# A post-norm decoder layer in float32: self-attention's division by the softmax sums moved from GpSimd to ScalarE, and a third buffer for rows of projections

## The chip, the cores and the metric

The kernel runs on one core of a Trainium2 chip. The metric is the time of one execution on the device, in microseconds (us). A core has five engines that work side by side, each through its own queue of instructions in order: TensorE (PE; its weight loads are listed as PEld), VectorE (DVE), ScalarE (ACT), GpSimd (POOL) and SyncE (SP, which here only issues DMAs). SBUF is the working memory on the core, PSUM the memory that TensorE writes its results to, DRAM the large memory outside.

## The reference, cut to what matters

Eight sequences of 256 tokens with 1024 features each go through one layer, all in float32. The layer is self-attention, cross-attention to a context, and a memory block, each followed by a residual sum and a layer norm:

```python
x = layernorm(x + self_attention(x))       # 32 heads of 32, 8 key/value heads, rope, causal
x = layernorm(x + cross_attention(x, ctx)) # 32 heads of 128, 8 key/value heads, rope, mask
x = layernorm(x + memory(x))               # router, top 8 of 256 slots, gate
```

The change touches the softmax of self-attention:

```python
attn = einsum('bhqd,bhkd->bhqk', q, k) * scale + causal
attn = softmax(attn, axis=-1)              # exp(a - max) / sum
out  = einsum('bhqk,bhkd->bhqd', attn, v)
```

## The kernel before

**Stages.** `run` calls `self_attention`, `cross_attention` and `tail`. Self-attention takes the first 1.3 ms of 3.7. Cross-attention needs keys and values projected from the context, and sums of blocks of its weights (it multiplies in Strassen's way, with seven products where eight would be plain). Both are made during self-attention, as filler for TensorE: `seven` (L625) makes the seven products p1 to p7, and `sums_of_inputs` and `sums_of_outputs` (L379, L397) let GpSimd add and subtract weight blocks (`combine`, L376 and L377) and write them to DRAM (L393, L413).

**Steps.** Self-attention runs 64 steps. Step s = 8b + c takes sequence b and chunk c of four heads. In step s the loop at L443 emits, in this order for TensorE:

- `transposed(s, 0)` to `transposed(s, 3)` (L283): three transposes per head of the softmax weights into one PSUM buffer `tr` (there is one), and a copy `at` out of it, by VectorE for heads 0 and 2, by ScalarE for heads 1 and 3 (L292). Between them lie single filler products (`one`) and `query(s + 2)`;
- `scores(s + 1)` (L241): the products of queries and keys of the next step, and their softmax;
- `others(s)` (L360): for c below 4 and b above 0 the output projection of the sequence before (L332), for c from 4 and b from 1 to 6 the keys (L195) or values (L223) of the next sequence. With c = 5 and 6 also `turn`, the transposes of the normed rows (L351), whose result ScalarE's queue writes to DRAM as `x1T` (L358);
- `weighted(s)` (L295): weights by values, and the copy `sa_oT` (L310) by VectorE;
- the rest of the filler. Steps 4 to 59 have four products of filler each.

TensorE's order is the one in which the program is written (`manual_schedule(engines={PE})`). On the other engines a scheduler of the language places the instructions, and each engine then runs its own in order.

**PSUM buffers.** Projections, outputs and filler products share three `mm` buffers in rotation. A product may start when the third allocation before it has been read by whoever copies it: ScalarE copies projections of queries and keys (`sa_raw`, L200), values (`sa_v`, L227) and the filler's first products (`half`, L665), VectorE the others.

**The softmax of a step.** The four heads form two tiles `att` of 128 x 2 x 384: for each head, 128 weights of the first block of queries and 256 of the second. For each of the eight parts VectorE takes scores, mask and maximum in one instruction (L265), and ScalarE the exponential with its sum (L270). For each tile VectorE forms the reciprocals of four sums (`rec`, L274), and GpSimd multiplies, two instructions per tile, each over both heads:

```python
rec = rec.rearrange("p (j t) -> p j t", t=2)
for i, (lo, hi) in enumerate(((0, 128), (128, 384))):
    nc.gpsimd.tensor_tensor(
        att[:, :, lo:hi], att[:, :, lo:hi],
        rec[:, :, i : i + 1].to_broadcast([P, 2, hi - lo]), ALU.mult,
    )
```

GpSimd's queue also holds the weight sums (L377), the last addition of rope (L623), the power in the layer norm (`ln_rstd`, L130), and DMA issues: residual rows (L117), rows of the position table (L572), keys (L722) and values (L727) on their way to DRAM.

**`raw`.** In `seven` VectorE assembles each result of 128 x 512 in a tile `raw` (L657), with two buffers. For keys and queries rope reads it. For values it is written to DRAM as it stands, by a DMA from GpSimd's queue, and its buffer is free when that write has landed.

Of the kernel before, what the change touches and what calls it, by code (L numbers as in the profile page):

```python
# [8 lines left out]
F32 = mybir.dt.float32  # L9
I32 = mybir.dt.int32  # L10
U32 = mybir.dt.uint32
AF = mybir.ActivationFunctionType
ALU = mybir.AluOpType
# [5 lines left out]
P = 128  # L19
# [16 lines left out]
TQ = 512  # L36
# [32 lines left out]
class Layer:  # L69
# [70 lines left out]
    def self_attention(self):  # L140
# [4 lines left out]
        nc, tc, a, uni, small = self.nc, self.tc, self.a, self.uni, self.small  # L145
# [95 lines left out]
        def scores(s):  # L241


            b, c = divmod(s, KC)
            qT, kT = qTs.pop(s), kTs[b]
            scs = [p_sc.tile([P, 2, 512], F32, name="sc") for _ in range(2)]
            for lo, hi, q0 in ((0, 128, 0), (128, 384, 128)):
                for j in range(4):
                    r = 32 * j
                    nc.tensor.matmul(  # L250
                        scs[j // 2][:, j % 2, lo:hi],
                        lhsT=qT[r : r + 32, q0 : q0 + P],
                        rhs=kT[r : r + 32, c // 4, 0 : hi - lo],
                        start=True, stop=True,
                    )
            atts[s] = []
            for sc in scs:
                att = sp.tile([P, 2, 384], F32, name="att", bufs=4)
                nmax = small.tile([P, 4], F32, name="nmax")
                sums = small.tile([P, 4], F32, name="sums")  # L260
                rec = small.tile([P, 4], F32, name="rec")
                parts = [(jj, lo, hi) for jj in range(2) for lo, hi in ((0, 128), (128, 384))]
                for i, (jj, lo, hi) in enumerate(parts):

                    nc.vector.tensor_tensor_reduce(  # L265
                        out=att[:, jj, lo:hi], in0=sc[:, jj, lo:hi], in1=mask[:, 256 - (hi - lo) :],
                        scale=-SA_SCALE, scalar=BIG, op0=ALU.add, op1=ALU.min,
                        accum_out=nmax[:, i : i + 1],
                    )
                    nc.scalar.activation(  # L270
                        att[:, jj, lo:hi], att[:, jj, lo:hi], AF.Exp,
                        bias=nmax[:, i : i + 1], scale=-1.0, accum_out=sums[:, i : i + 1],
                    )
                nc.vector.reciprocal(rec, sums)  # L274
                rec = rec.rearrange("p (j t) -> p j t", t=2)
                for i, (lo, hi) in enumerate(((0, 128), (128, 384))):
                    nc.gpsimd.tensor_tensor(  # L277
                        att[:, :, lo:hi], att[:, :, lo:hi],
                        rec[:, :, i : i + 1].to_broadcast([P, 2, hi - lo]), ALU.mult,
                    )  # L280
                atts[s].append(att)

# [154 lines left out]
        values(0, 0)  # L437
        query(1)
        scores(0)
        values(0, 1)  # L440
        last = SA_STEPS
        later = None
        for s in range(last):  # L443
# [34 lines left out]
            if s + 1 < last:  # L478
                scores(s + 1)
# [145 lines left out]
    def seven(self, name, m, xb, turned, done, eager=False):  # L625

        nc = self.nc
        now = {}  # L630
        if eager:
            now["a"] = self.weights([P, KC, XA_D], self.a[name][2 * m])

        def product(w, block):
            ps = self.mm()
            rhs = xb()[block]
            if turned:
                for t in range(2):
                    for k in range(4):
                        nc.tensor.matmul(  # L640
                            ps[:, t * P : (t + 1) * P], lhsT=rhs[:, k, t * P : (t + 1) * P], rhs=w[:, k, :],
                            start=(k == 0), stop=(k == 3),
                        )
            else:
                for k in range(4):
                    nc.tensor.matmul(  # L646
                        ps[:, :S], lhsT=w[:, k, :], rhs=rhs[:, k, :], start=(k == 0), stop=(k == 3)
                    )
            return ps[:, :S]

        def add(out, in0, in1):
            nc.vector.tensor_tensor(out, in0, in1, ALU.add)  # L652

        def half():
            return self.hp.tile([P, S], F32, name="half", bufs=4)

        def raw():  # L657
            return self.uni.tile([P, TQ], F32, name="raw", bufs=2)

        def p1():  # L660
            if not eager:
                now["a"] = self.weights([P, KC, XA_D], self.a[name][2 * m])
            ps = product(now["a"][:, :4, :], "B11")
            now["p1"] = half()
            nc.scalar.copy(now["p1"], ps)  # L665

        def p2():
            ps = product(now["a"][:, 4:, :], "B21")
            now["c1"] = raw()
            add(now["c1"][:, :S], ps, now["p1"])  # L670

        def p6():
            now["s24"] = self.weights([P, KC, XA_D], self.wsums[name, m][0])
            ps = product(now["s24"][:, :4, :], "T2")
            now["u2"] = half()
            add(now["u2"], ps, now["p1"])

        def p7():
            now["s31"] = self.weights([P, KC, XA_D], self.wsums[name, m][1])
            ps = product(now["s31"][:, :4, :], "T3")  # L680
            now["u3"] = half()
            add(now["u3"], ps, now["u2"])

        def p5():
            ps = product(now["s31"][:, 4:, :], "T1")
            now["c2"] = raw()
            add(now["u2"], ps, now["u2"])
            add(now["c2"][:, S:], ps, now["u3"])

        def p3():  # L690
            ps = product(now["s24"][:, 4:, :], "B22")
            add(now["c1"][:, S:], ps, now["u2"])
            done(0, now["c1"])

        def p4():
            w = self.weights([P, 4, XA_D], self.a[name][2 * m + 1][:, 4:, :])
            ps = product(w, "T4")
            add(now["c2"][:, :S], ps, now["u3"])
            done(1, now["c2"])

        return [p1, p2, p6, p7, p5, p3, p4]
# [680 lines left out]
```

## Time and profile before

| what | value |
|---|---|
| runs | 3705.0, 3705.7, 3714.4 us (median 3705.7) |
| the profiled execution's own time | 3709.3 us |
| its span, first to last instruction | 3707.5 us |
| mean granted TensorE clock | 0.974 of full speed |
| GpSimd's divisions (L277) | 256 instructions, 211.9 us |
| ScalarE's exponentials (L270) | 512 instructions, 225.3 us |
| SP's queue waiting for writes of `x1T` | 88.1 us, 13 times |

The profile is one execution taken by the hardware profiler. A group of instructions is given by its line in the kernel, its engine and operation, what it writes and reads, its number, its busy time, the mean duration of one in ns, and the idle time of the engine before it with what ended that. A line of waits says who waited for whom, for how many us in all, how often, and the longest. A line of the timeline gives the start in us, the duration, the engine and the instruction, and in brackets how long the engine had been idle and what released it. A line of windows gives, for a stretch of the span, its length, then the busy time and number of instructions on PE, PEld, DVE, ACT and POOL, the mean granted clock, the share of DMA time and GB/s. TensorE's records count two matmuls for one of the program in float32, transposes apart. The granted clock is TensorE's[...].

### The profile page before, as it was taken

How to read it: one execution, taken by the hardware profiler on the slowest of the kernel's cores; microseconds unless marked ns; L12 is line 12 of the kernel's file. 1: busy time of each engine (PE TensorE's matmuls, PEld its weight loads, DVE VectorE, ACT ScalarE, POOL GpSimd, SP SyncE). 2: the span in 40 equal slices, each digit the busy share in tenths (PEclk: the TensorE clock that was granted, in tenths of full speed). 3: DMA queues.
4: the chain of work that ended last, by engine and by line, in shares of the span. 5: the costliest groups of instructions: out<-in, count | busy, mean ns of one | idle time of the engine just before them, and what ended most of it. 6: DMA issues, size and time to landing. Idle time of an engine off the chain costs nothing.

```text
span 3707.5 us, 48946 instructions
## 1 busy us (share of the span) xinstructions
PE 3556.7 (96%) x17422; PEld 2614.0 (71%) x17422; DVE 2059.2 (56%) x5874; ACT 943.3 (25%) x2905; POOL 982.0 (26%) x1007
## 2 busy tenths in 40 slices
PE   6999999899999889999999999999999999999997
PEld 5777777676768657777777777777767777777764
DVE  4555555554655444555565555656565566455567
ACT  2322222222222213222222222222222222222223
POOL 4445454545544211111121111211111111111110
PEclk8999999999999989999999999999999999999996
DMA  7547575756665353333433333432433443333322
GB/s 263 181 168 256 196 264 209 248 195 226 241 218 177 118 203 116 123 120 117 150 125 127 119 109 120 149 129 100 136 112 120 141 132 117 122 112 117 117 87 114
DMA packets 220642, 574.18 MB, mean 155 GB/s; under 512 B 21104, under 2 KB 57264, under 8 KB 218992
## 3 DMA queue, kind: packets, MB, share of 16 engines
q1 hardware_dynamic: 173504, 461.26, 37.6%
q0 software_dynamic: 22528, 77.61, 5.6%
q10 hardware_dynamic: 24368, 32.18, 2.4%
q8 instruction: 139, 2.28, 0.2%
q14 instruction: 103, 0.84, 0.1%
HBM read 478.31 MB, written 92.67 MB: 154 GB/s over the span
## 4 chain that ended last, share of the span: by engine, by line
PE 66%; DVE 4%; POOL 1%; DMA 1%; issue 1%; ACT 1%; SPq 0%; POOLq 0%; ACTq 0%; DVEq 0%
PE mm L646 20%; PE mm L844 19%; PE sc L746 6%; PE mm L795 5%; PE tr L779 3%; PE mm L332 2%; PE mm L195 2%; PE mm L1079 2%; PE mm L640 1%; PE mm L1219 1%; PE mm L1073 1%; PE mm L899 1%; PE tr L287 1%; POOL acc L872 0%; DVE res L872 0%
## 5 line engine op out<-in xcount | busy, mean ns | idle before, releaser
L646 PE MATMUL mm<-x1T,w 128*128 128x256 f32 x3584 | 846.4, 381 | 10.8 <-DMA w<-xa_wq_sums 5.8
L646 PEld LDWEIGHTS mm<-x1T,w 128*128 128x128 f32 x3584 | 672.9, 191 | 102.5 <-issue 15.1
L623 POOL TENSOR_TENSOR qT<-qT,t 128x512 f32<-128x512 f32 x128 | 162.8, 1272 | 1120.9 <-DVE t L622 855.0
L844 PE MATMUL mm<-w,xoS 128*128 128x512 f32 x992 | 447.7, 594 | 0.0
L760 ACT ACTIVATE xatt<-xatt,nmax 128x256 f32<-128x256 f32 x512 | 255.5, 500 | 489.3 <-DVE nmax L755 477.2
L652 DVE TENSOR_TENSOR raw<-mm,half 128x256 f32<-128x256 f32 x384 | 161.5, 421 | 378.4 <-PE mm L646 310.0
L844 PE MATMUL mm<-w,xoT 128*128 128x512 f32 x744 | 335.1, 593 | 0.0
L652 DVE TENSOR_TENSOR half<-mm,half 128x256 f32<-128x256 f32 x288 | 121.6, 422 | 359.3 <-PE mm L646 300.9
L844 PEld LDWEIGHTS mm<-w,xoS 128*128 128x128 f32 x992 | 181.4, 190 | 182.8 <-issue 174.9
L277 POOL TENSOR_TENSOR att<-att,rec 128x256 f32<-128x256 f32 (+1 forms) x256 | 211.9, 849 | 332.2 <-DVE rec L274 325.9
L746 PE MATMUL sc<-kT,qT 128*128 128x256 f32 x1024 | 264.5, 382 | 6.9 <-POOL qT L623 6.7
L270 ACT ACTIVATE att<-att,nmax 128x128 f32<-128x128 f32 (+1 forms) x512 | 225.3, 441 | 147.9 <-DVE nmax L265 147.9
L795 PEld LDWEIGHTS mm<-xat,v 128*128 128x128 f32 x1024 | 194.0, 190 | 81.8 <-issue 57.9
L195 PE MATMUL mm<-xT,w 128*128 128x256 f32 x1024 | 245.3, 395 | 0.0
L795 PE MATMUL mm<-xat,v 128*128 128x256 f32 x1024 | 242.4, 379 | 1.5 <-ACT xat L784 1.5
L640 PE MATMUL mm<-w,ctxT 128*128 128x128 f32 x1792 | 227.0, 284 | 10.7 <-ACT sa_v L227 10.1
L844 PEld LDWEIGHTS mm<-w,xoT 128*128 128x128 f32 x744 | 138.9, 190 | 138.6 <-issue 119.9
L332 PE MATMUL mm<-sa_wo,sa_oT 128*128 128x512 f32 x512 | 229.8, 602 | 0.0
L640 PEld LDWEIGHTS mm<-w,ctxT 128*128 128x128 f32 x1792 | 216.8, 199 | 17.2 <-ACT sa_v L227 11.5
L810 POOL TENSOR_TENSOR xoS<-xoT 128x512 f32<-128x512 f32 x62 | 78.5, 1266 | 567.9 <-ACT xoT L804 567.9
L784 ACT COPY xat<-tr 128x512 f32<-128x512 f32 x256 | 148.0, 582 | 308.3 <-PE tr L779 308.0
L755 DVE CUSTOM_DVE_ANT_0 xatt<-sc,bias 128x256 f32<-128x256 f32 x512 | 196.4, 420 | 45.2 <-PE sc L746 38.8
(198 smaller groups left out, 5068.0 us busy)
## 6 DMA issues: line engine op xcount, KB each, us to landing
w<-in_xa_wo SPq DMA_DIRECT2D x129, 512.0 KB, 4.0
w<-xa_wq_sums SPq DMA_DIRECT2D x128, 512.0 KB, 3.4
w<-xa_wo_sums SPq DMA_DIRECT2D x124, 512.0 KB, 3.4
w<-in_xa_wq SPq DMA_DIRECT2D x96, 512.0 KB, 3.5
w<-in_sa_wq SPq DMA_DIRECT2D x64, 512.0 KB, 6.7
sa_wo<-in_sa_wo SPq DMA_DIRECT2D x64, 512.0 KB, 6.0
w<-xa_wk_sums SPq DMA_DIRECT2D x32, 512.0 KB, 4.6
w<-xa_wv_sums SPq DMA_DIRECT2D x32, 512.0 KB, 5.7
```

Source lines behind the costliest of these rows:

```text
L195: nc.tensor.matmul(ps[:, :S], lhsT=lhs[:, k, :], rhs=xT[:, k, :], start=(k == 0), stop=(k == KC - 1),)
L270: nc.scalar.activation(att[:, jj, lo:hi], att[:, jj, lo:hi], AF.Exp, bias=nmax[:, i : i + 1], scale=-1.0, accum_out=sums[:, i : i + 1],)
L277: nc.gpsimd.tensor_tensor(att[:, :, lo:hi], att[:, :, lo:hi], rec[:, :, i : i + 1].to_broadcast([P, 2, hi - lo]), ALU.mult,)
L332: nc.tensor.matmul(ps, lhsT=oTs[b * KC + c][:, tt * P : (tt + 1) * P], rhs=wos[b, half][c // 2][:, c % 2, :], start=(c == 0), stop=(c == K ...
L640: nc.tensor.matmul(ps[:, t * P : (t + 1) * P], lhsT=rhs[:, k, t * P : (t + 1) * P], rhs=w[:, k, :], start=(k == 0), stop=(k == 3),)
L646: nc.tensor.matmul(ps[:, :S], lhsT=w[:, k, :], rhs=rhs[:, k, :], start=(k == 0), stop=(k == 3))
L652: nc.vector.tensor_tensor(out, in0, in1, ALU.add)
L746: nc.tensor.matmul(sc[:, qt, :], lhsT=qT[:, q0 : q0 + P], rhs=kT[:, b * S : (b + 1) * S], start=True, stop=True,)
L755: nc.vector.tensor_tensor_reduce(out=att[:, qt, :], in0=sc[:, qt, :], in1=self.bias[:, 2 * b + qt, :], scale=-XA_SCALE, scalar=BIG, op0=AL ...
L760: nc.scalar.activation(att[:, qt, :], att[:, qt, :], AF.Exp, bias=nmax[:, qt : qt + 1], scale=-1.0, accum_out=sums[:, qt : qt + 1],)
L795: nc.tensor.matmul(po[:, b * S : (b + 1) * S], lhsT=self.v[G][:, NB * b + kt, :], rhs=at[:, kt * S : (kt + 1) * S], start=(kt == 0), stop= ...
L844: nc.tensor.matmul(ps, lhsT=oT[lhs][:, u, off + p * P : off + (p + 1) * P], rhs=w[:, u, :], start=(u == 0), stop=(u == 1),)
```

## The change

ScalarE multiplies by the reciprocals, with an Identity activation whose scale is the column of `rec`: four instructions per tile, one per head and block of queries, in place of GpSimd's two. And `raw` has three buffers in place of two.

```diff
@@ -272,11 +272,9 @@
                 nc.vector.reciprocal(rec, sums)
-                rec = rec.rearrange("p (j t) -> p j t", t=2)
-                for i, (lo, hi) in enumerate(((0, 128), (128, 384))):
-                    nc.gpsimd.tensor_tensor(
-                        att[:, :, lo:hi], att[:, :, lo:hi],
-                        rec[:, :, i : i + 1].to_broadcast([P, 2, hi - lo]), ALU.mult,
+                for i, (jj, lo, hi) in enumerate(parts):
+                    nc.scalar.activation(
+                        att[:, jj, lo:hi], att[:, jj, lo:hi], AF.Identity, bias=0.0, scale=rec[:, i : i + 1]
                     )
                 atts[s].append(att)
@@ -655,7 +653,7 @@
         def raw():
-            return self.uni.tile([P, TQ], F32, name="raw", bufs=2)
+            return self.uni.tile([P, TQ], F32, name="raw", bufs=3)
```

## The prediction

> **What bounds the kernel now.** I read the page first (parts 1 and 2), then the waits, then the timeline of single steps of self-attention.
>
> ```profile
> PE 3556.7 (96%) x17422; PEld 2614.0 (71%) x17422; DVE 2059.2 (56%) x5874; ACT 943.3 (25%) x2905; POOL 982.0 (26%) x1007
> ...
> 100.00:1330.00 1230.00, 1150.66 (x7349) 890.11 (x7349) 667.79 (x2089) 324.87 (x1228) 562.56 (x635) 0.97 0.60 209
> ...
> L277 POOL TENSOR_TENSOR att<-att,rec 128x256 f32<-128x256 f32 (+1 forms) x256 | 211.9, 849 | 332.2 <-DVE rec L274 325.9
> ...
> PE tr L287 <- DVE at L292: 41.0, 21, 9.8
> ...
> PE tr L287 <- POOL att L277: 29.0, 21, 6.3
> ```
>
> TensorE sets the end: busy for 96% of the span. The windows line gives 100 to 1330 us, most of self-attention: PE 1150.7 of 1230 us (so 79 us idle), ACT 325, POOL 563. ScalarE has room by its sum, GpSimd is the fuller one. So the change is worth what it does to PE's idle time there (about 102 us from 25 to 1330 us, adding PE's gaps along the timeline) and nothing else. Of that, 29.0 us ended when a GpSimd division landed, 41.0 us when VectorE emptied the one `tr` buffer.
>
> The second reading is of one step with filler. It shows what ScalarE must do in time:
>
> ```profile
> 614.57 0.94 PE L250 MATMUL sc<-sa_kT,sa_qT 32*128 32x128 f32 x16
> 615.44 3.72 PE L195 MATMUL mm<-xT,wk 128*128 128x256 f32 x16
> 616.81 0.40 ACT L270 ACTIVATE att<-att,nmax 128x128 f32<-128x128 f32 x1 [1.60 <-DVE nmax L265]
> 617.12 0.19 ACT L270 ACTIVATION_READ_ACCUMULATOR att<-att,nmax 128x1 f32 x1
> 617.21 0.49 ACT L270 ACTIVATE att<-att,nmax 128x256 f32<-128x256 f32 x1
> ...
> 620.34 0.34 ACT L200 COPY sa_raw<-mm 128x256 f32<-128x256 f32 x1
> 620.42 0.40 PE L305 MATMUL mm<-at,sa_v 128*32 128x128 f32 x8
> ...
> 620.75 1.99 PE L646 MATMUL mm<-ctxT,w 128*128 128x256 f32 x8
> ...
> 838.34 0.35 ACT L227 COPY sa_v<-mm 128x256 f32<-128x256 f32 x1
> 838.74 0.48 PE L646 MATMUL mm<-ctxT,w 128*128 128x256 f32 x1 [1.54 <-ACT sa_v L227]
> ...
> 862.48 1.25 POOL L377 TENSOR_TENSOR w<-w 128x512 f32<-128x512 f32 x1 [9.74 <-DMA w<-in_xa_wo]
> ...
> 865.28 0.48 PE L287 MATMUL tr<-ident,att 128*128 128x128 f32 x1 [3.74 <-POOL att L277]
> ```
>
> The eight exponentials of a step run without a break (616.81 to 620.3), then ScalarE copies the key projection out of PSUM (`sa_raw`, L200), and PE's next product starts 0.06 us after that copy, because it reuses that `mm` buffer (three in rotation). PE rides on ScalarE here with no slack. At 838.7 PE even waited 1.54 us for such a copy. The last two lines show GpSimd's fault: its queue stood 9.74 us behind a combination waiting for a DMA, and the division behind it held PE for 3.74 us.
>
> **What the Trainium skill says.** "ScalarE: Activation LUTs", What ACT_TABLE_LOAD costs: an ACTIVATE with one pointer operand takes 280 ns + 0.833 ns per element, about 93 ns more for a second pointer, and neighbours overlap by about 93 ns. The trace agrees: exponentials of 128 and 256 elements take 0.39 and 0.49 us (387 and 493 by that formula), the next instruction starting 0.09 us before the end. "SBUF — State Buffer", Who interferes with whom: a VectorE instruction with two SBUF inputs is blocked by a GpSimd one that reads SBUF, ScalarE by nobody. The trace agrees: L209 takes 0.42 us alone and 0.9 to 1.16 us beside L277. "TensorE: Matmul & The Clock Gate", HAM oscillation: idle gaps over about 3.4 us drop PE to half clock. Here the stretches with the 9.8 us and 3.7 us gaps show clocks of 0.95 and 0.94; lone gaps of about 1.5 us left no half-clock record after them.
>
> **The change part by part.** Step s = 8b + c has batch row b, chunk c.
>
> *The move.* 256 GpSimd multiplications (211.9 us) go; 512 Identity activations come, four to each half step. One has an immediate bias and one pointer (`rec`), like the exponential without its accumulator: start to start 0.30 and 0.40 us, so four take D = 1.40 us. 128 fours add 179 us to ScalarE. If each carried two pointers or did not overlap, D would be 1.77; nothing makes it lower. No table load is added: the built program has 15 before and after.
>
> *The order.* The instruction order of the built program is unchanged on PE and SP. ScalarE's step was eight exponentials, copies; it is now six exponentials, four Identity, two exponentials, the copy of keys or values, four Identity, other copies. So every copy that PE waits for comes 1.40 us later. On VectorE the second reciprocal moves behind the copy of `sa_oT` or `turn` in steps with c >= 4; it too is 1.40 us later, since its sums come from the last two exponentials.
>
> *Cost, c = 4 to 7, b = 1 to 6 (24 steps: keys and values of the next row).* From the end of the copy to the product that reuses its buffer the timeline has: c=4: 1.07 to 1.13 us; c=5: 0.05 to 0.07; c=6: 0.17 or 0.18; c=7: 0.05, PE already waiting, 11.8 us in all (0.2, 0.9, 4.3, 1.5, 2.7, 2.2). The least gap is 0.05. So c=4: 6 x 0.35 = 2.1; c=5: 6 x 1.39 = 8.3; c=6: 6 x 1.28 = 7.7. For c=7 the exponentials were late since VectorE's rope stood beside GpSimd's weight sums (L377): unchanged lateness costs 6 x 1.40 = 8.4 us more; lateness gone leaves 6 x 0.36 = 2.2, a gain of 9.6. GpSimd's run of sums should end 1.5 to 3 us sooner but not vanish: I take +2.
>
> *Cost elsewhere.* Steps 3 and 4 have no filler, and transposes 1 and 2 wait for `at` copies now behind the late reciprocal and the second four: +1.0 each. Step 27, where scores came late, lets L337 free its buffer 1.4 us later: +1.3. In other steps with c < 4 the output projection (7.1 us on PE) covers both fours; without it they too would cost 1.4 us each. Sum of costs: 18.1 + 2 + 3.3 = 23.4 us.
>
> *Gains.* Step 0: GpSimd took up the divisions at 39.74 and 44.83, though the sums' reciprocals began at 35.14 and 37.62, behind L377 and DMA issues; ScalarE would have the first piece at about 36.3, so transpose 0 comes 4.2 us sooner, and about 2 us more from transpose 2, less what step 1 gives back: 6. Step 41: the 3.74 + 0.51 us wait goes, and with it some 6.8 us at half clock worth 3: 7. In steps 35 and 43 `ln_rstd` (L130) stood behind two divisions (1.6 us) with PE waiting (9.8 and 3.2 us; the DMA wait ahead of them stays): 3.2. Step 48, rope beside a division: 1.3. Steps 5 to 8: the second half division was late by 0.4 to 0.7, net 1.7. Steps 61 and 63: 1.1. Sum 20.3. Nearly all else that GpSimd loses lies beside PE work. VectorE loses about 13 us of blocking (92 us in all, 59 beside L377), mostly off the path.
>
> *The third `raw` buffer.* VectorE waited three times, 13.8 us, for a values buffer whose write to DRAM was not done (246.8, 828.0, 1132.1). No PE gap follows any of them: 0, at best 3. Cross-attention uses `raw` too, but rope frees it at once.
>
> *DMAs moved.* Writes of `x1T` from ScalarE's queue (`turn`) are issued 2.8 us later, and SP waits for them before reusing a weight slot (13 times). PE's weights of this stretch landed over 5 us before use but for two loads, so nothing is taken; if that cover were short, each late load would cost up to 2.8.
>
> *Net:* +23.4 - 20.3 = +3 us on the profiled execution (3709.3 us, span 3707.5): 3712. The median of the runs shown is 3705.7, so 3709.
>
> **Rivals.** *No change that can be told* (forecast): both sums of about 20 us cancel, within 11 us (0.3%, about what a measurement of this kernel can tell from no change). *Slower:* one mechanism, ScalarE's copies of keys and values behind the first four. All four c at full price is 2.1 + 8.3 + 7.7 + 8.4 = 26.5, plus about 4 where c=7's gaps pass the clock gate, plus 3.3, less only 10 of the gains: +24, 3730. It decides as soon as the gains stay under about 23 us (33.8 - 11), or at D = 1.77. For it: the 0.05 us slack, certain; the gains hang on where GpSimd's queue happens to stand. *Faster:* GpSimd, free of divisions, finishes its sums before the rope of c=7, and that wait goes (-9.6); VectorE's blocking and the clock recover another 6: 18.1 + 3.3 - 9.6 - 26.3 = -14.5, 3691. For it: GpSimd 46% busy and strictly in order; against: L377, the larger blocker, stays. That the change does not do what it says is ruled out by the built order.
>
> **How the numbers follow.** No change 0.50, slower 0.32, faster 0.18. Predicted 3709. The likeliest case alone is 3696 to 3717. To leave out no more than 2 in 10, I go down to 3694 and up to the slower case's 3730.
>
> **What would show it.** Right: Identity 0.39 and 0.49 us; PE waits on `sa_raw` (L200) and `sa_v` (L227) up from about 12 us to 30 or so; "PE tr <- POOL att" gone and a few us of "PE tr <- ACT att" left; cross-attention after 1330 us of the same length. Wrong: those waits below 15 us (c=7 recovered, faster); new PE waits for a weight's DMA or for `at`, or a clock below 0.97 in 100 to 1330 us (slower).

## The result, and the profile after

The changed kernel takes 3689.28 us (median of 5 runs, 3680.62 to 3689.79) against 3705.7 us before (5 runs, 3702.56 to 3714.42): ratio 0.9945, 95% interval 0.9928 to 0.9962. It is faster by 16.4 us, outside the range that was forecast (3694 to 3730). The profiled execution took 3687.42 us with a span of 3685.7, 21.8 less than the span before. In what follows line numbers past the division are two lower than before (L287 is now L285, L292 is L290, L646 is L644), and the division, L277 before, is L276.

From the page of the changed kernel, engines' busy time:

```profile
PE 3547.3 (96%) x17422; PEld 2605.7 (71%) x17422; DVE 2027.9 (55%) x5874; ACT 1122.8 (30%) x3417; POOL 767.6 (21%) x751
```

ScalarE gained 180 us and GpSimd lost 214, near the 179 and 212 of the prediction; VectorE lost 31, where the prediction had about 13. The price of one division is in the groups by form from 93 to 1300 us (busy us, mean ns of one | idle before):

```profile
L276 ACT ACTIVATE att<-att,rec 128x256 f32<-128x256 f32 x240 | 118.5, 494 | 0.0
L276 ACT ACTIVATE att<-att,rec 128x128 f32<-128x128 f32 x240 | 93.7, 391 | 8.8 <-DVE rec L274 8.5 <-issue 0.2
```

391 and 494 ns are within 1.1% of the 387 and 493 that were worked out from the formula of the Trainium skill ("ScalarE: Activation LUTs", What ACT_TABLE_LOAD costs). Four in a row take 1.48 us to the end of the last, and what follows them starts 1.38 us after the first (609.78 after 608.40 below), where 1.40 was forecast. So the cost of the new instructions was right. The windows line for 100 to 1330 us (duration, then PE, PEld, DVE, ACT, POOL, clock, DMA share, GB/s) shows where the time is not:

```profile
100.00:1330.00 1230.00, 1157.05 (x7367) 887.49 (x7366) 644.47 (x2093) 492.81 (x1707) 364.50 (x397) 0.98 0.60 210
```

PE is busy for 6.4 us more of the same window at a clock of 0.98 in place of 0.97. The scores of the last step (63) begin at 1286.4 us and no longer at 1310.6; from there to the end it is 2399.3 us after and 2396.9 before. All of the gain lies in self-attention. Adding PE's gaps over 0.12 us along the timeline, from 25 us to the end of that stage, as the prediction did: 101.8 us before, 88.4 after. The waits (idle us, times, longest) name what is left. For `sa_v` the kernel before had:

```profile
PE mm L640 <- ACT sa_v L227: 10.1, 4, 4.3
PE mm L646 <- ACT sa_v L227: 1.7, 2, 1.5
```

and the changed kernel has:

```profile
PE tr L285 <- DVE at L290: 38.5, 17, 8.1
PE tr L285 <- ACT att L276: 13.8, 8, 3.5
PE mm L638 <- ACT sa_v L227: 11.7, 4, 4.1
PE mm L644 <- ACT sa_v L227: 3.5, 2, 2.9
```

The 29.0 us that PE waited for GpSimd's divisions have become 13.8 us for ScalarE's. The waits for `sa_v` (c=7) rose from 11.8 to 15.2. What is missing is a line for `sa_raw`, L200: the prediction had PE wait for it in every step with c=5 and for `sa_v` in every step with c=6, 16.0 us in all. The timeline after the scores of step 30 began at 603.62 (they are issued in step 29, so the copy is of c=5) shows why not:

```profile
608.40 1.48 ACT L276 ACTIVATE att<-att,rec 128x128 f32<-128x128 f32 x4
...
609.47 0.40 PE L303 MATMUL mm<-at,sa_v 128*32 128x128 f32 x8
609.78 0.39 ACT L270 ACTIVATE att<-att,nmax 128x128 f32<-128x128 f32 x1
609.80 3.50 PE L644 MATMUL mm<-ctxT,w 128*128 128x256 f32 x15
...
610.66 0.35 ACT L200 COPY sa_raw<-mm 128x256 f32<-128x256 f32 x1
```

The first four divisions stand ahead of the last two exponentials, and the copy of `sa_raw` begins 7.04 us after those scores; before it was 5.77 (620.34 after 614.57). So the copy is late by 1.27 us, near the 1.40 forecast. But PE's first filler product starts at 609.80, ahead of the copy. Before, the product came after it (620.75 after a copy from 620.34). The product no longer uses the buffer that this copy empties. In the traces its first matmul waits for a semaphore of ScalarE before, and for one of VectorE now; the second filler product waits for ScalarE instead, and by the time it starts, eight records or some 1.8 us after the first, the copy is done (611.01). It is so in all twelve steps with c=5 and 6 (b=1 to 6): in the changed kernel the first filler product starts 6.18 us after the scores in each of them, without a gap. TensorE's 17422 records come in the same order, with the same tiles, in both traces. What moved is which of the three `mm` buffers the pool hands to which product. So the rule given ahead of the prediction, that a product waits for the reader of the third allocation before it, doesn't hold for the changed kernel.

In step 0 the wait went as forecast. Before:

```profile
39.74 1.62 POOL L277 TENSOR_TENSOR att<-att,rec 128x256 f32<-128x256 f32 x2
40.43 0.47 PE L287 MATMUL tr<-ident,att 128*128 128x128 f32 x1 [6.34 <-POOL att L277]
```

and after:

```profile
35.55 1.61 POOL L570 DMA_INDIRECT w<-in_xa_table,pos_u  x1 [0.30 <-issue]
35.79 1.48 ACT L276 ACTIVATE att<-att,rec 128x128 f32<-128x128 f32 x4
36.23 1.06 PE L285 MATMUL tr<-ident,att 128*128 128x128 f32 x3 [2.92 <-ACT att L276]
37.19 1.55 POOL L375 TENSOR_TENSOR w<-w 128x512 f32<-128x512 f32 x1
```

ScalarE divides while GpSimd is still at its gathers and sums; before, the division came behind both, at 39.74, and PE waited for 6.34 us. In step 41 GpSimd still stands for a weight, but PE isn't behind it:

```profile
841.21 1.47 ACT L276 ACTIVATE att<-att,rec 128x128 f32<-128x128 f32 x4
...
845.94 1.26 POOL L375 TENSOR_TENSOR w<-w 128x512 f32<-128x512 f32 x1 [8.42 <-DMA w<-in_xa_wo]
```

### The profile page after: what moved, and what is told of

Its sections match the earlier page's. It is cut to its first block, busy times and chain, and to the rows that moved or that the text cites. A ratio compares the mean times of both kernels' runs of the same rounds, so it can differ in the third digit from the quotient of the medians.

```text
span 3685.7 us, 48839 instructions
## 1 busy us (share of the span) xinstructions
PE 3547.3 (96%) x17422; PEld 2605.7 (71%) x17422; DVE 2027.9 (55%) x5874; ACT 1122.8 (30%) x3417; POOL 767.6 (21%) x751
## 4 chain that ended last, share of the span: by engine, by line
PE 78%; DVE 5%; ACT 2%; DMA 2%; POOL 2%; issue 1%; SPq 0%; POOLq 0%; ACTq 0%; DVEq 0%
PE mm L644 23%; PE mm L842 19%; PE sc L744 6%; PE mm L793 5%; PE mm L330 5%; PE mm L195 5%; PE mm L638 4%; PE tr L777 3%; PE mm L1077 2%; PE tr L285 2%; ACT att L270 1%; PE mm L1217 1%; PE mm L1071 1%; PE sc L250 1%; PE mm L897 1%
## 5 line engine op out<-in xcount | busy, mean ns | idle before, releaser
L644 PE MATMUL mm<-x1T,w 128*128 128x256 f32 x3584 | 847.6, 382 | 8.0 <-DMA w<-xa_wq_sums 4.9
L644 PEld LDWEIGHTS mm<-x1T,w 128*128 128x128 f32 x3584 | 673.0, 191 | 99.7 <-issue 12.3
L802 ACT COPY xoT<-mm 128x512 f32<-128x512 f32 x128 | 74.9, 585 | 568.2 <-PE mm L793 568.2
L744 PEld LDWEIGHTS sc<-kT,qT 128*128 128x128 f32 x1024 | 194.0, 192 | 36.9 <-POOL qT L621 9.8
```

What stands on the lines that cost most here:

```text
L644: nc.tensor.matmul(ps[:, :S], lhsT=w[:, k, :], rhs=rhs[:, k, :], start=(k == 0), stop=(k == 3))
L744: nc.tensor.matmul(sc[:, qt, :], lhsT=qT[:, q0 : q0 + P], rhs=kT[:, b * S : (b + 1) * S], start=True, stop=True,)
```

## The experiments

Theory A: the gain comes from taking the divisions out of GpSimd's in-order queue, and the price on ScalarE wasn't paid in c=5 and 6 because the pool dealt the `mm` buffers differently. The rivals are named with each run.

### The two parts apart

The changed kernel with two slots again:

```diff
-            return self.uni.tile([P, TQ], F32, name="raw", bufs=3)
+            return self.uni.tile([P, TQ], F32, name="raw", bufs=2)
```

and the kernel before with three:

```diff
-            return self.uni.tile([P, TQ], F32, name="raw", bufs=2)
+            return self.uni.tile([P, TQ], F32, name="raw", bufs=3)
```

> The division on ScalarE, raw with two slots as before. Theory A (the gain is the division leaving GpSimd's in-order queue): the time of the changed kernel, 3686 to 3694 us; PE idles some 14 us less than before in self-attention and the half-clock stretches are shorter. Rival B (the gain is the third raw slot, which takes away VectorE's three waits of 13.8 us in all): 3700 us or more.

> The third raw slot alone, the division on GpSimd as before. Theory A: 3702 to 3709 us, the time of before, though VectorE's three waits for the slot's DMA go. Rival B: 3686 to 3694 us.

Measured: the division alone 3683.94 us, ratio 0.994 (0.9927 to 0.9953); the slot alone 3704.63 us, ratio 0.9999 (0.9989 to 1.0009). The division is the whole gain; the slot is worth nothing that can be told. Rival B falls.

### The pool's buffers in a fixed rotation

Three pools of one buffer, taken in turn, in place of one pool of three:

```diff
-        self.p_mm = [self.pool("mm", 3, space=PSUM)] * 3
+        self.p_mm = [self.pool(f"mm{i}", 1, space=PSUM) for i in range(3)]
```

> The changed kernel with the three mm buffers in a fixed rotation (three pools of one buffer each). Theory A (ScalarE's copies of keys and values do come 1.4 us late, and it cost nothing in steps with c=5 and 6 because the pool gave the first filler product there the buffer that VectorE empties): 12 products now wait about 1.3 us each for L200 and L227, so 15 to 18 us more than the changed kernel, 3702 to 3708 us, and in step 30 the first filler product starts after the copy of sa_raw, near 7.4 us after the step's scores and not at 6.2. Rival C (the copies' lateness lies beside other work in any rotation): 3686 to 3694 us.

> The kernel before with the same fixed rotation, as the control of the run above: every theory expects the time of before, 3702 to 3709 us, since the first filler product already used the buffer that ScalarE's copy frees.

Measured: 3698.51 us, ratio 0.9981 (0.997 to 0.9991) for the changed kernel with the fixed rotation; the control 3705.53 us, ratio 0.9998 (0.999 to 1.0006). Before the change the fixed rotation costs nothing. After it it costs 14.6 us against the division alone (two slots), measured side by side with it, and 9.2 us against the first five runs of the changed kernel (three slots). A's range was missed by 3.5 us, and so were its 15 to 18 us of difference, both on the low side; the direction is A's and clear of noise. The profile is of an execution of 3714.06 us, the slowest of eleven, so its waits serve to find the place and not to add up the time:

```profile
PE mm L638 <- ACT sa_v L227: 12.9, 6, 3.3
PE mm L644 <- ACT sa_v L227: 7.7, 5, 2.9
PE mm L638 <- ACT sa_raw L200: 4.4, 3, 2.1
PE mm L644 <- ACT sa_raw L200: 3.6, 3, 1.2
```

The timeline of that execution in the same place (the scores of step 30 began at 611.26):

```profile
617.10 0.40 PE L303 MATMUL mm<-at,sa_v 128*32 128x128 f32 x8
...
617.80 0.49 ACT L270 ACTIVATE att<-att,nmax 128x256 f32<-128x256 f32 x1
618.29 0.35 ACT L200 COPY sa_raw<-mm 128x256 f32<-128x256 f32 x1
...
618.70 3.72 PE L644 MATMUL mm<-ctxT,w 128*128 128x256 f32 x16 [1.19 <-ACT sa_raw L200]
```

The copy stands where it stood in the changed kernel, 7.03 us after the scores and behind two exponentials, and now PE stands behind it and goes on at 7.44 us, as A had it. In the gaps by step this 1.19 us turns up on top in 11 of the 12 steps with c=5 and 6, and 0.90 in the twelfth: 14.0 us that the profile of the division alone doesn't have. Rival C falls: what spared PE the late copy was the buffer that the product was dealt.

### Where the division goes, and in how many steps

The changed kernel with all divisions on VectorE:

```diff
-                    nc.scalar.activation(
-                        att[:, jj, lo:hi], att[:, jj, lo:hi], AF.Identity, bias=0.0, scale=rec[:, i : i + 1]
+                    nc.vector.tensor_scalar(
+                        att[:, jj, lo:hi], att[:, jj, lo:hi], rec[:, i : i + 1], None, ALU.mult
                     )
```

and with ScalarE in four steps, GpSimd in the others:

```diff
+                if s in (0, 35, 41, 43):
+                    for i, (jj, lo, hi) in enumerate(parts):
+                        nc.scalar.activation(
...
+                else:
+                    rec = rec.rearrange("p (j t) -> p j t", t=2)
+                    for i, (lo, hi) in enumerate(((0, 128), (128, 384))):
+                        nc.gpsimd.tensor_tensor(
...
```

> The changed kernel with the division on VectorE (tensor_scalar) in place of ScalarE. Theory A (what paid was leaving GpSimd's queue, whose turn can stand behind a weight's DMA; which engine takes the division matters less): the waits of steps 0 and 41 go here too, and the time is 3685 to 3698 us. Rival E (VectorE, 55% busy and owner of the copies that empty tr and mm, becomes the bound when it gets some 2.6 us more per step): 3705 us or more, with PE waiting longer for the copies of L290.

> ScalarE divides in steps 0, 35, 41 and 43 alone; GpSimd divides in the other 60, as before; three raw slots. Theory A (the gain lies in a few places where GpSimd's queue stood): of PE's idle time, step 0 gives about 6, step 41 about 4 and step 35 up to 2 us, and with the half clock that followed them the time is 3687 to 3698 us. Rival D (the gain is spread over all steps, since VectorE is no longer blocked by 256 divisions): 3702 us or more.

Measured on VectorE: 3703.15 us, ratio 0.9991 (0.9984 to 0.9998). A was wrong here, and rival E is near. PE's waits for VectorE's copies grew from 38.5 to 51.5 us:

```profile
PE tr L285 <- DVE at L290: 51.5, 22, 9.6
PE tr L285 <- DVE att L276: 12.3, 7, 3.1
```

and PE waited ten times, 9.9 us in all, for VectorE's copy of a `turn` (L350), which it did not do in the changed kernel. PE's gaps come to 102.0 us, as many as before the change. Leaving GpSimd isn't enough: here the engine that took the work also makes the copies that PE waits for most. ScalarE empties `tr` for as many heads as VectorE, but in the changed kernel PE waited 6.3 us for its copies and 38.5 for VectorE's.

Measured with four steps on ScalarE: 3695.46 us, ratio 0.9971 (0.9959 to 0.9982), so 11 of the 16 to 22 us that the full change gave, within A's range and below D's. Four steps of 64 bring half or more, and yet not the whole: the fault shows again at other divisions left on GpSimd. In the profile, of an execution of 3701.93 us, the slowest of seven, the four steps have 11.9 us less of gaps than before and the other steps 11.5 us more. The timeline of this kernel in step 1 (5.1 us of PE's gaps in the changed kernel, 9.5 here):

```profile
52.25 1.25 POOL L383 TENSOR_TENSOR w<-w 128x512 f32<-128x512 f32 x1 [3.46 <-DMA w<-in_xa_wk]
...
58.93 1.61 POOL L283 TENSOR_TENSOR att<-att,rec 128x256 f32<-128x256 f32 x2
...
59.61 0.47 PE L293 MATMUL tr<-ident,att 128*128 128x128 f32 x1 [7.54 <-POOL att L283]
```

The sums begin 3.46 us late for a weight's DMA, the division comes behind the last of them at 58.93, and PE has waited for 7.54 us. It is the same queue and the same reason as in steps 0 and 41.

### ScalarE later by another four passes

```diff
+                if len(atts[s]) == 0:
+                    for i, (jj, lo, hi) in enumerate(parts):
+                        nc.scalar.activation(att[:, jj, lo:hi], att[:, jj, lo:hi], AF.Identity, bias=0.0, scale=1.0)
```

> The changed kernel with four more Identity passes (scale 1.0) after the first four of each step, so that ScalarE's copies come another 1.4 us late. Theory A: the first filler product in c=5 and 6 still uses VectorE's buffer and pays nothing, but the waits for sa_v in c=7 grow by about 1.4 us in each of 6 rows and steps 0 to 4 by about 1 us each: 10 to 16 us more than the changed kernel, 3696 to 3705 us. Rival C (ScalarE's lateness is covered everywhere): under 3692 us. If the copies of c=5 and 6 are paid after all: 3712 us or more.

Measured: 3701.48 us, ratio 0.9987 (0.9977 to 0.9998). The number is in A's range, 12 us over the changed kernel, but not for A's reason. The waits for `sa_v` did not grow, they shrank from 15.2 to 4.4 us:

```profile
PE mm L641 <- ACT sa_v L227: 3.2, 3, 1.2
PE mm L647 <- ACT sa_v L227: 1.2, 1, 1.2
```

In this program the product that waited in c=7 waits for VectorE in all six rows: it was dealt VectorE's buffer. Of the extra gaps, 1.9 us lie in steps 3 and 4 and 1.5 in step 0 as expected, but step 1 lost 1.5; PE's waits for ScalarE's Identity passes and copies of `tr` grew from 20.1 to 31.2 us; over all, PE's gaps are 95.9 us (88.4 without the passes), and the stretches before 1330 us in which the trace has TensorE's granted clock at half sum to 99 us (75). One part of A came true: in c=5 and 6 the first filler product still waits for VectorE, and in 11 of the 12 steps it starts 6.18 us after the scores, without a gap. For the rest this run is no proof of A; it shows once more that an edit on ScalarE moves the buffers.

### Taking the last of ScalarE's late copies away

```diff
-            nc.scalar.copy(vs[b][:, tt, :], ps[:, :256])
+            (nc.vector.tensor_copy if b and tt else nc.scalar.copy)(vs[b][:, tt, :], ps[:, :256])
```

> The changed kernel with the second copy of values out of PSUM (L227, c=7) on VectorE in place of ScalarE. Theory A (the 15.1 us for which PE still waits in c=7 are ScalarE's copy standing behind the exponentials and the first four Identity): VectorE makes that copy right after its first reciprocal, PE's waits for sa_v fall under 4 us, and the time is 3672 to 3681 us, below both kernels. Rival: the product behind it is late anyway (its weights or the buffer's other reader), 3685 us or more.

> The kernel before with the second copy of values (L227, c=7) on VectorE. Theory A: in this program both reciprocals of a step stand ahead of that copy on VectorE, and the second waits for all eight exponentials, so the copy is as late as ScalarE's was: PE still waits some 8 to 14 us for sa_v and the time is that of before, 3701 to 3709 us. Rival (the copy on VectorE is worth the same with either kernel): 3694 to 3699 us.

> The changed kernel once more, beside the runs of this call, to set the other edits against it: 3683 to 3691 us by every theory; PE's waits for sa_v about 15 us in c=7 and none for sa_raw above 0.2 us in c=5 and 6.

Measured on the changed kernel: 3680.58 us (3670.16 to 3683.64), ratio 0.9924 (0.9909 to 0.9939), within A's range. The changed kernel again, measured later: 3688.88 us, ratio 0.9954 (0.994 to 0.9968), with waits for `sa_v` of 12.7 us. The version with the copy on VectorE has the lowest median here, by 8 us against the changed kernel, whose interval lies above its own in these later runs, but by 3.4 us only against the division alone with two slots (3683.94 us, 0.9927 to 0.9953), with whose interval its own overlaps. Its waits:

```profile
PE tr L285 <- DVE at L290: 48.4, 21, 8.8
...
PE mm L638 <- DVE sa_v L227: 1.7, 2, 1.4
```

13.5 of the 15.2 us for `sa_v` went, but 9.9 us more are waits for VectorE's copies of `tr` than in the profile of the changed kernel (in step 32 PE's gaps are 5.7 us against 4.6, in step 43 5.3 against 4.5). Whether the edit causes these was not tried. In all, PE's gaps are 81.9 us here, and 88.4 and 81.0 in the two profiles of the changed kernel: that the wait for `sa_v` went is shown, that its going is the whole of the gain is not. The same line put into the kernel before gives 3706.28 us, ratio 1.0002 (0.9994 to 1.001), with the waits as long as they were:

```profile
PE mm L640 <- DVE sa_v L227: 9.2, 4, 2.9
PE mm L646 <- DVE sa_v L227: 2.3, 2, 1.8
```

There both reciprocals of the step stand ahead of the copy on VectorE, and the second waits for all eight exponentials; in the changed kernel the second reciprocal comes behind the copy. The edit gained only with the order of instructions that the change brought.

## Why the prediction was wrong

The forecast was the sum 23.4 - 20.3 = +3 us. The gains were about right (17.3 of the 20.3 us were gaps of PE, and the places named lost 13.3 and 16.7 in the two profiles of the changed kernel; the other 3 us were clock). The costs were not. Waits for `sa_raw` and `sa_v` near 30 us were to show that the prediction held; they are 15.2 and 12.7.

- **The step that failed** is in Cost, c = 4 to 7. The second reading has PE's next product start 0.06 us after the copy "because it reuses that `mm` buffer (three in rotation)", which is right for the kernel before; Cost carries this over to the changed kernel, so that each copy that is 1.40 us late holds PE for that much. The copies were late, but the rotation didn't stay. In the changed program the pool gave the first filler product the buffer that VectorE empties; why it deals so is not shown, only that an edit on ScalarE changed it. The 8.3 + 7.7 us for c=5 and 6 were 0 in the changed kernel. With the rotation that the prediction assumed they were 14.0, so the size was nearly right for that rotation. The prediction compared the order of instructions and took the unchanged order on PE to mean unchanged waits.
- **c=4:** 2.1 us predicted; the gaps there grew by 0.14 us or less each.
- **c=7:** 11.8 us and +2 predicted; 15.2 and 12.7 in the two profiles of the changed kernel. About right, and the wait did not vanish, so the faster rival (3691), which had that wait go, had the time nearly right for another reason than its own.
- **Steps 3, 4 and 27:** +1.0, +1.0, +1.3 predicted; +0.8, +0.8, and for step 27 +1.5 in one profile and -0.9 in the other.
- **Step 0:** -6 predicted; the gaps fell from 10.9 to 5.1. **Step 41:** the 4.25 us went entirely, and the half-clock stretch behind them too.
- **Steps 35 and 43:** -3.2 predicted. 9.8 became 8.1 and 9.5, and 3.2 became 4.5 and 3.0: little or nothing. The sum of weights ahead of `ln_rstd` waits for a DMA there, divisions or not. The changed kernel's timeline in step 35, whose 8.1 us are PE's longest wait in this stage:

```profile
725.08 1.26 POOL L375 TENSOR_TENSOR w<-w 128x512 f32<-128x512 f32 x1 [9.35 <-DMA w<-in_xa_wo]
...
727.21 0.59 POOL L130 TENSOR_TENSOR ln_rstd<-ln_ve,neghalf 128x1 f32<-128x1 f32 x1
```

- **Steps 5 to 8:** -1.7 predicted, -0.4 and -1.7 in the two profiles. **Step 48:** -1.3 predicted, -1.3 and -2.8. **Steps 61 and 63:** -1.1 predicted, -1.0.
- **The third slot:** 0 predicted, 0 measured (1 us, interval across no change), though VectorE's three waits for the slot's DMA are gone.

Without the 18.1 us for c=4 to 6 the sum would have been 2 + 3.3 - 20.3 = -15, so 3694 us on the profiled execution and 3691 against the median: 1.4 us from what was measured. That is partly luck, since the misses in steps 35 and 43 are made up elsewhere. Three profiles with GpSimd's divisions (before, the slot alone, the control) have 102.9 us of gaps in the mean and reach the scores of step 63 at 1306.6; three with ScalarE's (the changed kernel twice, the division alone) have 86.6 and reach them at 1285.2. So 16.3 of 21.4 us are gaps. In the means of the same profiles PE's waits for the division fell from 29.0 to 12.1 us, those for VectorE's copies of `tr` from 42.1 to 39.5, and those for `sa_v` rose from 11.1 to 14.6. That adds up to 16.0, about the 16.3 of the gaps, and it is the division's own wait that brings it; a VectorE less held up by GpSimd, rival D of the run with four steps, is worth 2.6 us at most in these copies. The other 5 us of the 21.4 fit the shorter stretches at half clock (76 us in the mean, not 101, from 25 to 1330 us), but no run isolates them, and this stays open.

## What to carry to other kernels

An unchanged order of instructions on an engine doesn't mean unchanged waits: where a pool hands out buffers, look up for each instruction on the path which engine frees the buffer it was given, in the changed program too, before a late copy is charged to it. Small pieces of work that the bound engine waits for were badly placed in an in-order queue that also waits for DMAs, though that queue's engine was idle for most of the time; and no better on the engine whose copies the bound engine waits for most. After such a move, try the other copies again: one that gained nothing before the change went with a median lower by 3 to 8 us after it.

## What the runs showed of the hardware

The prediction reckoned with half clock after idle gaps over about 3.4 us, the figure that it cites; the traces have it after shorter ones too, and they decide here. In the profile of before, PE stood idle for 1.91 us from 428.94, and a half-clock record (a stretch with the granted clock at half) of 3.4 us begins at 430.9; it stood idle for 2.01 us from 2534.45, and one begins at 2536.9. Another gap of 2.01 us, from 1965.86, has none behind it. So the length of a gap alone doesn't tell here whether the clock falls.

What half-clock time costs stays open. From the scores of step 63 to the end, the twelve profiles took 2395.8 to 2400.3 us, with 78.7 to 89.5 us of half-clock records in that stretch. Those with more took somewhat longer, about 0.4 us for 1 us (correlation 0.8). In self-attention 25 us less of it goes with at most the 5 us that the gaps leave over. No run changes the clock alone, so neither number is a price.
